# Second layer of a graph attention network on one core: tiles in ascending order of in-edges, a softmax in two halves for the largest three, and a later start of the next tile's softmax

## The chip, the cores and the metric

The kernel runs on one core of one Trainium2 chip, as one launch. The metric is the device time of that core in microseconds (us); less is better. The profile is of one execution, whose time is given beside the median.

## The reference, cut to what matters

A graph of 10000 nodes with 768 numbers each has 160000 edges, drawn at random in both directions, to which the kernel's input already adds one self loop for each node; the network adds another one. Two graph attention layers follow, with float32 throughout:

```python
def gat_conv(x, edge_index, W, a_src, a_dst, bias, heads, out_ch, concat):
    ei = _add_self_loops(edge_index, n)
    src, dst = (ei[0], ei[1])
    xl = (x @ W).reshape(n, heads, out_ch)
    e = leaky_relu(alpha_src[src] + alpha_dst[dst], 0.2)   # a dot of xl with a_src, a_dst
    m = jax.ops.segment_max(e, dst, num_segments=n)
    e = jnp.exp(e - m[dst])
    s = jax.ops.segment_sum(e, dst, num_segments=n)
    alpha = e / (s[dst] + 1e-16)
    msg = xl[src] * alpha[:, :, None]
    out = jax.ops.segment_sum(msg, dst, num_segments=n)
    return out + bias

h = layer_norm(gat_conv(x, ..., W1, HEADS=4, HID=256, concat), g1, be1)
h1 = relu(h) + (x @ Wr1 + br1)
h = layer_norm(gat_conv(h1, ..., W2, 1 head, OUT_DIM=768), g2, be2)
out = _layernorm(x + h + (h1 @ Wr2 + br2))
```

For each node, then, the rows of its in-neighbours are fetched, weighed by a softmax over their logits, and summed. In layer 2 such a row has 768 numbers, and two more for the logits.

## The kernel before

**Tiles and slots.** The kernel sorts the nodes by their number of in-edges and puts 128 of them, one on each partition, into each of 79 tiles (`NT`). A tile with at most n in-edges on a node has n slots, also called rows here: slot k of a tile holds the k-th in-neighbour of each of its 128 nodes, a transfer of 128 rows of 770 float32, 394 KB. The numbers of slots are fixed beforehand: 41, 27, 26, 25, 24 twice, 23 twice, 22 four times, 21 four times, 20 six times, 19 seven times, 18 seven times, 17 eight times, 16 seven times, 15 eight times, then fewer, down to 8; 1377 (`TOTAL`) in all. `SLOTS[t]` is the number of tile t, `FIRST[t]` its first slot.

**The order of the tiles.** Both layers go through the tiles in one order, every other size upwards and the remaining sizes downwards: 8, 10, 11 and so on up to 24, 26, 41, and then 27, 25, 24, 23 and so on down to 11, 11, 9. `TURNS[t]` is the place of tile t in the sorted list.

**Layer 2.** `ordered_layer2` keeps a ring of 41 slots (`RING2`) in SBUF. The instruction order of all engines is the program's own. `Ring.fetch` (L449) issues the transfer of a slot once the slot's former row has been used: slot 0 of a tile (the node's own row) by a plain DMA of SyncE (SP), every other by an indirect DMA of GpSimd (POOL), in `gather` (L424). 1298 gathers go through POOL's queue in this layer, and between them the 79 scatters of the results (L970). A gather whose slot is not yet free waits at the head of that queue.

For each tile of n rows, this is done:

- `weights_of` first makes the n logits and their exponentials (`logits`, L477 to L485; it needs all n rows in the ring), and at its second step the normalised weights (`normalised`, L496 to L499).
- Of each row, 512 columns are multiplied by the weight and summed on VectorE (DVE), one instruction a row (`weigh`, L519). The other 256 columns are summed in PSUM by TensorE (PE) with a diagonal matrix of the weights (L938); ScalarE (ACT) makes each diagonal from the identity (L937), in 5 buffers (`DIAGONALS`) of 4 diagonals each.
- `residual` (L949, L952) puts x and h1 @ Wr2 into other columns of the same PSUM tile; SP loads what it needs (L903, L904).
- `norms` makes the two layer norms: the deviation (`deviation`, L577 to L582, whose `sd` is made by ACT), then `scaled` (L591, L593) and the residual (L962), then the second deviation, the output (L968) and the scatter (L970). Its steps are issued in the next tile, ahead of row 0 and at rows 3, 6 and 9.

A row's ring slot is free when both the DVE's `weigh` and PE's diagonal matmul have read it.

**Where the next tile's softmax starts.** While tile t of n rows is weighed, the next tile's weights are made ahead. With `LEAD` = 3:

```python
if t + 1 < NT and SLOTS[t + 1] + LEAD <= ring.size:
    ahead = weights_of(t + 1)
    turn = min(max(n // 3, n + SLOTS[t + 1] + 2 * LEAD - ring.size), n - LEAD)
```

At row `turn` DVE's queue gets the next tile's logits, at row `turn` + 3 its normalised weights, and ACT and PE get its diagonals. A tile of 41 rows fills the whole ring, so its softmax is not made ahead: it comes after the last row of the tile before it.

Of the kernel before, what the change touches and what calls it, by code (L numbers as in the profile page):

```python
# [28 lines left out]
F32 = mybir.dt.float32  # L29
I32 = mybir.dt.int32  # L30
BF16 = mybir.dt.bfloat16
AF = mybir.ActivationFunctionType
# [13 lines left out]
G = 4  # L46
# [4 lines left out]
ON_PE2 = 512  # L51
SHARE = 4
ON_PE1 = 4


def chunk_counts(n_edges):
# [23 lines left out]
def gnn_kernel(ctx, tc, x, x_cols, src, dst, src_col, dst_col, W1, a_src1, a_dst1, b1, g1, be1, Wr1, br1,  # L80
# [342 lines left out]
    def gather(to, table, index, **more):  # L423
        nc.gpsimd.indirect_dma_start(out=to, out_offset=None, in_=table,  # L424
                                     in_offset=bass.IndirectOffsetOnAxis(ap=index, axis=0), **more)
# [14 lines left out]
    class Ring:  # L440
# [1 line left out]

        def __init__(self, pool, table, row, size, own):
            self.table, self.size, self.own, self.issued = table, size, own, 0
            self.rows = pool.tile([P, size, row], F32, name="ring")

        def fetch(self, upto):  # L449
            for q in range(self.issued, min(upto, TOTAL)):  # L450
                if q in self.own:
                    nc.sync.dma_start(self.slot(q), self.table[self.own[q] * P:(self.own[q] + 1) * P, :])
                elif q < self.size or self.own:
                    gather(self.slot(q), self.table[:, :], slots[:, q:q + 1])
                else:
                    gather(self.slot(q), self.table[:, :], slots[:, q:q + 1], bounds_check=NP - 1,
                           oob_is_err=False)
                self.issued = q + 1
# [12 lines left out]
    def logits(small, ring, lo, hi, ad, heads, c, top=None):  # L471


        n = hi - lo
        e = small.tile([P, ring.size, heads], F32, name="e")[:, :n]
        for a, b, rows in ring.parts(lo, hi):
            nc.vector.tensor_tensor(e[:, a - lo:b - lo], rows[:, :, c + heads:c + 2 * heads],  # L477
                                    ad[:, None, :].to_broadcast([P, b - a, heads]), op=OP.add)
        leaky(e, e)
        new = small.tile([P, heads], F32, name="new")  # L480
        nc.vector.reduce_max(new, e.rearrange("p k h -> p h k"), axis=AX.X)
        if top is not None:
            nc.vector.tensor_max(new, new, top)
        nc.vector.tensor_tensor(e, e, new[:, None, :].to_broadcast([P, n, heads]), op=OP.subtract)  # L484
        nc.scalar.activation(e, e, AF.Exp)  # L485
        for a, b, rows in ring.parts(lo, hi):
            if not ring.own:
                nc.vector.tensor_scalar(slots[:, a:b], rows[:, :, R1 - 1], -1.0, float(NP), op0=OP.mult, op1=OP.min)
                nc.vector.memset(rows[:, :, c + heads:], -BIG)
        return e, new  # L490

    def normalised(small, e, heads, t):

        doubled(e, t)
        total = small.tile([P, heads], F32, name="total")
        nc.vector.reduce_sum(total, e.rearrange("p k h -> p h k"), axis=AX.X)  # L496
        nc.vector.tensor_scalar(total, total, 1e-16, None, op0=OP.add)
        nc.vector.reciprocal(total, total)
        nc.vector.tensor_mul(e, e, total[:, None, :].to_broadcast([P, e.shape[1], heads]))  # L499
# [176 lines left out]


    SLOTS, FIRST = [SLOTS[t] for t in TURNS], [FIRST[t] for t in TURNS]

    def nodes(t):  # L680
        return order[:, TURNS[t]:TURNS[t] + 1]
# [195 lines left out]

    def ordered_layer2():
        nonlocal ps_big
        with tc.tile_pool(name="b2", bufs=1) as pool, tc.tile_pool(name="small2", bufs=2) as small, \  # L880
                tc.tile_pool(name="ps_acc2", bufs=2, space=PSUM) as ps_acc, \
                tc.tile_pool(name="ps_q2", bufs=3, space=PSUM) as ps_big, tc.manual_schedule():
# [1 line left out]
            wr2 = wr1.rearrange("p k n -> p (k n)")[:, :K1 * C2].rearrange("p (k n) -> p k n", n=C2)  # L884
            load(wr2, Wr2)
            parts = pieces(w2.rearrange("p k n -> p (k n)")[:, :6 * C1], C1)
            ring = Ring(pool, table2, R2, RING2, dict(zip(FIRST, TURNS)))

            rest, flat = RING2 * R2, ring.rows.rearrange("p k n -> p (k n)")

# [9 lines left out]
            def fetch_x(t):  # L900

                hT, xt = firsts[t] if t < 2 else (parts[t % 2], parts[2 + t % 2][:, :D0])
                nc.sync.dma_start(hT, h1_d[t])  # L903
                nc.sync.dma_start(xt, x_d[t])  # L904
                return hT.rearrange("p (k n) -> p k n", n=P), xt

            ins = {0: fetch_x(0)}
# [9 lines left out]
            ones = pool.tile([1, P], F32, name="ones")  # L917
            nc.vector.memset(ones, 1.0)

            def whole(t):  # L920
                return SLOTS[t] <= ring.size

            def weights_of(t):


                n = SLOTS[t]
                ad = small.tile([P, H2], F32, name="ad")
                nc.vector.tensor_add(ad, ring.slot(FIRST[t])[:, C2:C2 + H2], lift)
                e, _ = logits(small, ring, FIRST[t], FIRST[t] + n, ad, H2, C2)
                yield e  # L930
                normalised(small, e, H2, t)
                to = rs[t][:, C2:2 * C2 - ON_PE2]
                nc.tensor.matmul(to, ones, b2_b[0:1, ON_PE2:], start=False, stop=False, skip_group_check=True)
                for k in range(n):
                    if k % G == 0:
                        diagonals = pool.tile([P, G, P], F32, name="diagonals", bufs=DIAGONALS)
                    nc.scalar.activation(diagonals[:, k % G, :], ident, AF.Copy, scale=e[:, k, :])  # L937
                    nc.tensor.matmul(to, diagonals[:, k % G, :], ring.slot(FIRST[t] + k)[:, ON_PE2:C2],  # L938
                                     start=False, stop=(k == n - 1), skip_group_check=True)
                yield  # L940

            def residual(t):

# [13 lines left out]
            def norms(t, h, r, means):  # L957

                stats = deviation(small, [a for m in means for a in pieces(m, C2 - ON_PE2)])
                yield  # L960
                scaled(h, means, stats, g2_b, be2_b)
                nc.vector.tensor_add(h, h, r[:, :C2])  # L962
                mean, inv = deviation(small, pieces(h, C2 // 2))
                yield
                less = small.tile([P, 1], F32, name="less")
                nc.vector.scalar_tensor_tensor(less, mean, -1.0, inv, op0=OP.mult, op1=OP.mult)
                o = pool.tile([P, C2], F32, name="out")
                nc.scalar.activation(o, h, AF.Identity, bias=less, scale=inv)  # L968
                yield
                nc.gpsimd.indirect_dma_start(  # L970
                    out=out, out_offset=bass.IndirectOffsetOnAxis(ap=nodes(t), axis=0),
                    in_=o, in_offset=None, bounds_check=N - 1, oob_is_err=False)

            assert C2 % BANK and C2 % BANK + C2 - ON_PE2 <= BANK
            q = product(brT, wr2, C2)
            rs = {0: residual(0)}
            last = iter(())
            ready = []
            assert all(whole(t) for t in range(NT))
            for t in range(NT):  # L980
                n = SLOTS[t]
                if 0 < t < NT - 1:
                    rs[t + 1] = residual(t + 1)
                h = parts[4 + t % 2][:, :C2]
                e = (ready or list(weights_of(t)))[0]
                acc = ps_acc.tile([P, BANK], F32, name="acc")
                if not t:
                    rs[1] = residual(1)
                    ring.fetch(RING2)
                next(last, None)  # L990
                ready, ahead, turn = [], iter(()), n
                if t + 1 < NT and SLOTS[t + 1] + LEAD <= ring.size:

                    ahead = weights_of(t + 1)
                    turn = min(max(n // 3, n + SLOTS[t + 1] + 2 * LEAD - ring.size), n - LEAD)
                for k in range(n):
                    if k in (turn, turn + LEAD):
                        ready += itertools.islice(ahead, 1)
                    if k in (LEAD, 2 * LEAD, 3 * LEAD):
                        next(last, None)  # L1000
                    weigh(acc, ring.slot(FIRST[t] + k), e[:, k], ON_PE2, None if k else b2_b)
                    ring.fetch(FIRST[t] + k + 1 + ring.size)
                    if t + 2 < NT and k == n // 2:
                        ins[t + 2] = fetch_x(t + 2)
                ready += ahead
                for _ in last:
                    pass
                if not t:
                    nc.vector.tensor_add(be2_b, be2_b, adds[1])
                    nc.vector.tensor_add(be2_b, be2_b, q[:, :C2])  # L1010
                last = norms(t, h, rs[t], [acc, rs[t][:, C2:2 * C2 - ON_PE2]])
                if t + 2 < NT and t + 2 not in ins:
                    ins[t + 2] = fetch_x(t + 2)
# [272 lines left out]
```

## Time and profile before

| | |
|---|---|
| times of three runs | 5635.85, 5646.04 and 5645.9 us, median 5645.9 |
| the profiled execution's own time | 5629.25 us |
| its span in the profile | 5627.4 us, granted TensorE clock 0.927 |
| busy over the span | PE 87%, DVE 76%, POOL 58%, ACT 50% |
| layer 2 | from about 3437 us to the end, 2190 us |
| the group of 26, 41 and 27 rows | 4461.3 to 4631.4 us, 170.1 us |
| the five tiles ahead of it | 4283.8 to 4461.3 us, 177.5 us |

All windows below are counted from the start of the span. The profiled execution is 16.7 us below the median. PE's large share of busy time comes from layer 1 and its products more than from layer 2, so shares over the whole span don't tell what bounds layer 2.

### The profile page before, as it was taken

The numbers are of one execution on the slowest core, as the hardware profiler recorded it, in microseconds if no ns is written. First come the engines' busy times: TensorE is split into PE (matmuls) and PEld (weight loads), VectorE is DVE, ScalarE is ACT, GpSimd is POOL, SyncE is SP. The second block draws the span as 40 slices with busy tenths as digits, with TensorE's granted clock in tenths as the row PEclk, the third lists the DMA queues.
The fourth block names the chain that finished last, engine by engine and source line by source line (L and its number), as shares of the span: only waits on it lengthen the run. The fifth ranks groups of instructions, "written<-read, shape, count | busy, mean of one in ns | idle before, by whom it ended". The sixth has DMA issues, their size and how long they took to land. (4 is left out here: it accounts for less than half of the span.)

```text
span 5627.4 us, 59568 instructions
## 1 busy us (share of the span) xinstructions
PE 4889.5 (87%) x15191; PEld 2895.8 (51%) x15191; DVE 4288.7 (76%) x7729; ACT 2810.9 (50%) x8184; POOL 3236.3 (58%) x3159
## 2 busy tenths in 40 slices
PE   8999996999999875789999999998887747788898
PEld 3444443555555543455555555565555534555565
DVE  5783344999998887888999995887676656767787
ACT  3443343777788776778877763332222222222232
POOL 2447364556666555566665543666565656666663
PEclk9999998999999987899999999998888878889999
DMA  4333626999999987899999986998888878888885
GB/s 155 122 99 87 92 89 243 327 338 350 361 363 364 347 318 263 317 346 357 366 356 354 337 292 246 330 337 313 294 301 286 282 242 291 307 300 305 304 328 201
DMA packets 474306, 1591.37 MB, mean 283 GB/s; under 512 B 118327, under 2 KB 122487, under 8 KB 473958
## 3 DMA queue, kind: packets, MB, share of 16 engines
q0 software_dynamic: 322384, 1286.62, 64.5%
q1 hardware_dynamic: 149520, 297.43, 15.7%
q10 hardware_dynamic: 2054, 3.42, 0.2%
q8 instruction: 128, 2.10, 0.1%
q14 instruction: 220, 1.80, 0.1%
HBM read 1431.80 MB, written 177.29 MB: 286 GB/s over the span
## 5 line engine op out<-in xcount | busy, mean ns | idle before, releaser
L424 POOL DMA_INDIRECT ring<-table,slots x2675 | 2655.8, 993 | 1791.0 <-issue 518.8
L519 DVE SCALAR_TENSOR_TENSOR acc<-ring,e,acc 128x512 f32<-128x512 f32 (+1 forms) x2530 | 1578.4, 624 | 148.0 <-PE acc L733 48.6
L508 ACT ACTIVATE ring<-ring,e 128x256 f32<-128x256 f32 x3284 | 1338.6, 508 | 1.4 <-issue 1.4
L515 DVE TENSOR_TENSOR acc<-acc,ring 128x1024 f32<-128x1024 f32 x801 | 985.6, 1230 | 71.4 <-DVE acc L519 1.4
L952 PE MATMUL big<-wr,w 128*128 128x512 f32 (+1 forms) x2464 | 878.9, 502 | 139.8 <-issue 137.9
L938 PE MATMUL big<-ring,diagonals 128*128 128x256 f32 x2754 | 742.1, 428 | 206.0 <-issue 159.2
L171 PE MATMUL big<-w,xT 128*128 128x512 f32 x1896 | 825.9, 597 | 27.0 <-DMA w<-in_W_dram 10.4
L171 PE MATMUL big<-wr,xT 128*128 128x512 f32 x1896 | 833.5, 596 | 0.2 <-issue 0.2
L826 PE MATMUL half<-w,hT 128*128 128x512 f32 (+1 forms) x2528 | 830.4, 486 | 0.0
L938 PEld LDWEIGHTS big<-ring,diagonals 128*128 128x128 f32 x2754 | 586.4, 216 | 364.9 <-issue 232.7
L952 PEld LDWEIGHTS big<-wr,w 128*128 128x128 f32 x2464 | 482.3, 197 | 499.9 <-issue 468.9
L937 ACT ACTIVATE diagonals<-ident,e 128x128 f32<-128x128 f32 x1377 | 424.3, 388 | 617.2 <-remote 227.0
L826 PEld LDWEIGHTS half<-w,hT 128*128 128x128 f32 x2528 | 477.8, 189 | 372.3 <-issue 333.2
L733 PE MATMUL acc<-ring,diagonals 128*128 128x256 f32 x1912 | 481.8, 410 | 209.4 <-ACT diagonals L727 203.8
L171 PEld LDWEIGHTS big<-w,xT 128*128 128x128 f32 x1896 | 362.0, 192 | 486.6 <-issue 466.3
L171 PEld LDWEIGHTS big<-wr,xT 128*128 128x128 f32 x1896 | 356.7, 192 | 420.6 <-issue 420.5
L733 PEld LDWEIGHTS acc<-ring,diagonals 128*128 128x128 f32 x1912 | 388.8, 206 | 295.4 <-ACT diagonals L727 225.0
L581 ACT ACTIVATE sd<-mv,eps 128x1 f32<-128x1 f32 x237 | 69.4, 293 | 709.9 <-DVE mv L579 398.4
L727 ACT ACTIVATE diagonals<-ident,e 128x128 f32<-128x128 f32 x956 | 293.0, 387 | 204.2 <-DVE e L499 171.9
L665 DVE TENSOR_TENSOR scr<-big,ad_b 128x1024 f32<-128x1024 f32 x79 | 96.7, 1224 | 379.9 <-ACT row L662 348.1
L670 POOL TENSOR_TENSOR row<-row,none 128x1024 f32<-128x1024 f32 x79 | 187.1, 2368 | 266.6 <-ACT row L662 264.6
L485 ACT ACTIVATE e<-e 128x68 f32<-128x68 f32 (+29 forms) x160 | 38.2, 239 | 567.0 <-DVE e L484 302.0
(173 smaller groups left out, 3635.0 us busy)
## 6 DMA issues: line engine op xcount, KB each, us to landing
ring<-table,slots POOLq DMA_INDIRECT x2675
table<-row SPq DMA_DIRECT2D x79, 516.0 KB
h_d<-hT SPq DMA_DIRECT2D x79, 512.0 KB
w<-h_d SPq DMA_DIRECT2D x77, 512.0 KB
table<-row SPq DMA_DIRECT2D x79, 385.0 KB
ring<-table SPq DMA_DIRECT2D x79, 385.0 KB
xT<-in_x_cols_dram SPq DMA_DIRECT2D x79, 384.0 KB
x_d<-xt SPq DMA_DIRECT2D x79, 384.0 KB
```

The costliest lines, as they stand in the source:

```text
L171: nc.tensor.matmul(p[:, c:e], aT[:, j, :], w[:, j, c:e], start=(j == 0), stop=(j == k - 1))
L424: nc.gpsimd.indirect_dma_start(out=to, out_offset=None, in_=table, in_offset=bass.IndirectOffsetOnAxis(ap=index, axis=0), **more)
L508: nc.scalar.activation(row[:, s], row[:, s], AF.Copy, scale=e[:, h:h + 1])
L515: nc.vector.tensor_add(acc[:, :c], acc[:, :c], row[:, :c])
L519: nc.vector.scalar_tensor_tensor(acc[:, s], row[:, s], e[:, h:h + 1], (acc if first is None else first)[:, s], op0=OP.mult, op1=OP.add)
L670: nc.gpsimd.tensor_add(row[:, :C1], row[:, :C1], b1_b)
L727: nc.scalar.activation(diagonals[:, k * H1 + i, :], ident, AF.Copy, scale=e[:, k, i:i + 1])
L733: nc.tensor.matmul(acc[:, c:d], diagonals[:, k * H1 + i, :], ring.slot(q + k)[:, c:d], start=(k == 0 and c % BANK == 0), stop=(k == m - 1 ...
L826: nc.tensor.matmul(q, hT[:, j, :], w2[:, j, c:c + q.shape[1]], start=(j == 0), stop=(j == K1 - 1))
L937: nc.scalar.activation(diagonals[:, k % G, :], ident, AF.Copy, scale=e[:, k, :])
L938: nc.tensor.matmul(to, diagonals[:, k % G, :], ring.slot(FIRST[t] + k)[:, ON_PE2:C2], start=False, stop=(k == n - 1), skip_group_check=True)
L952: nc.tensor.matmul(r[:, c:d], hT[:, j, :], wr2[:, j, c:d], start=False, stop=(j == K1 - 1 and d < C2), skip_group_check=True)
```

## The change

Three things are changed, all in layer 2; layer 1 keeps its order and its code.

1. The tiles go from the fewest slots to the most: 8, 10, 11, 11, 9, 12 and so on up to 24, 24, and at the end 41, 25, 26, 27. (The two tiles that come last in layer 1 are sorted as if they had two slots more.) `Ring` gets a list `at` that maps the new order of slots to the columns of `slots`.
2. A tile of 26 or more rows (`PARTED2`) makes its softmax in two halves: 13 and 13, 20 and 21, 13 and 14 rows. After the first half the weights stay unnormalised; with the second half's maximum, `fade` rescales what both sums hold: ACT multiplies the 256 PSUM columns by it, and DVE the 512 columns of `acc` with one more instruction.
3. `turn` gets 4 * `LEAD` where it had 2 * `LEAD`, and counts the next tile's first half alone. For tiles of 18 rows it goes from row 6 to 7, of 19 from 6 to 9, of 20 from 6 to 11, of 21 from 7 to 13, of 22 from 9 to 15, of 23 from 11 or 12 to 17 and of 24 from 13 to 19. Up to 17 rows it stays where it was.

```diff
+PARTED2 = 26
...
-                    gather(self.slot(q), self.table[:, :], slots[:, q:q + 1])
+                    gather(self.slot(q), self.table[:, :], slots[:, self.at[q]:self.at[q] + 1])
...
     def ordered_layer2():
+        turns = sorted(range(NT), key=lambda t: SLOTS1[t] + 2 * (t >= NT - 2))
+        turns.insert(-3, turns.pop())
+        SLOTS = [SLOTS1[t] for t in turns]
+        FIRST = list(itertools.accumulate([0] + SLOTS[:-1]))
+        at = [FIRST1[t] + k for t in turns for k in range(SLOTS1[t])]
...
             def weights_of(t):
...
-                normalised(small, e, H2, t)
...
+                e, top = logits(small, ring, at, at + cuts[1], ad, H2, C2)
+                yield {0: (e, None)}
+                if len(cuts) == 2:
+                    normalised(small, e, H2, turns[t])
+                    add_b2()
+                else:
+                    doubled(e, turns[t])
+                    total = small.tile([P, H2], F32, name="total")
+                    nc.vector.reduce_sum(total, e.rearrange("p k h -> p h k"), axis=AX.X)
+                summed(e, 0, cuts[1])
                 yield
+                for lo, hi in zip(cuts[1:], cuts[2:]):
+                    e, new = logits(small, ring, at + lo, at + hi, ad, H2, C2, top)
+                    fade = small.tile([P, H2], F32, name="fade")
+                    nc.vector.tensor_sub(fade, top, new)
+                    nc.scalar.activation(fade, fade, AF.Exp)
+                    yield
...
+                    nc.vector.tensor_mul(e, e, total[:, None, :].to_broadcast([P, hi - lo, H2]))
+                    nc.scalar.activation(to, to, AF.Copy, scale=fade)
+                    add_b2()
+                    summed(e, lo, hi)
+                    yield lo, (e, fade)
...
-                    turn = min(max(n // 3, n + SLOTS[t + 1] + 2 * LEAD - ring.size), n - LEAD)
+                    turn = min(max(n // 3, cuts[-2] + 1, n + cuts_of(t + 1)[1] + 4 * LEAD - ring.size), n - LEAD)
                 for k in range(n):
+                    if k + LEAD in cuts[1:-1]:
+                        next(later)
+                    if k + 1 in cuts[1:-1]:
+                        lo, es_lo = next(later)
+                        es[lo] = es_lo
...
+                        if k == lo and fade is not None:
+                            nc.vector.scalar_tensor_tensor(acc[:, :ON_PE2], acc[:, :ON_PE2], fade, b2_b[:, :ON_PE2],
+                                                           op0=OP.mult, op1=OP.add)
```

More of the change, by code (lines that the diff above doesn't have):

```diff
@@ L440, in gnn_kernel, with __init__ @@
     class Ring:
-        def __init__(self, pool, table, row, size, own):
+        def __init__(self, pool, table, row, size, own, at=None):
             self.table, self.size, self.own, self.issued = table, size, own, 0
+            self.at = at or list(range(TOTAL))
             self.rows = pool.tile([P, size, row], F32, name="ring")
@@ L678, in gnn_kernel @@
     SLOTS, FIRST = [SLOTS[t] for t in TURNS], [FIRST[t] for t in TURNS]
+    SLOTS1, FIRST1 = SLOTS, FIRST
     def nodes(t):
@@ L886, in ordered_layer2 @@
             parts = pieces(w2.rearrange("p k n -> p (k n)")[:, :6 * C1], C1)
-            ring = Ring(pool, table2, R2, RING2, dict(zip(FIRST, TURNS)))
+            ring = Ring(pool, table2, R2, RING2, dict(zip(FIRST, (TURNS[t] for t in turns))), at)
             rest, flat = RING2 * R2, ring.rows.rearrange("p k n -> p (k n)")
@@ L902, in fetch_x @@
                 hT, xt = firsts[t] if t < 2 else (parts[t % 2], parts[2 + t % 2][:, :D0])
-                nc.sync.dma_start(hT, h1_d[t])
-                nc.sync.dma_start(xt, x_d[t])
+                nc.sync.dma_start(hT, h1_d[turns[t]])
+                nc.sync.dma_start(xt, x_d[turns[t]])
                 return hT.rearrange("p (k n) -> p k n", n=P), xt
@@ L918, in ordered_layer2, with cuts_of @@
             nc.vector.memset(ones, 1.0)
-            def whole(t):
-                return SLOTS[t] <= ring.size
+            def cuts_of(t):
+                n = SLOTS[t]
+                return [0, n // 2, n] if n >= PARTED2 else [0, n]
             def weights_of(t):
-                n = SLOTS[t]
+                n, at, cuts = SLOTS[t], FIRST[t], cuts_of(t)
                 ad = small.tile([P, H2], F32, name="ad")
-                nc.vector.tensor_add(ad, ring.slot(FIRST[t])[:, C2:C2 + H2], lift)
-                e, _ = logits(small, ring, FIRST[t], FIRST[t] + n, ad, H2, C2)
-                yield e
-                normalised(small, e, H2, t)
+                nc.vector.tensor_add(ad, ring.slot(at)[:, C2:C2 + H2], lift)
@@ L932, in weights_of @@
                 to = rs[t][:, C2:2 * C2 - ON_PE2]
[L933 to L939, printed above, removed]
@@ L940, in weights_of, with summed @@
-                yield
+                def summed(e, lo, hi):
+                    for k in range(lo, hi):
+                        if (k - lo) % G == 0:
+                            diagonals = pool.tile([P, G, P], F32, name="diagonals", bufs=DIAGONALS)
+                        nc.scalar.activation(diagonals[:, (k - lo) % G, :], ident, AF.Copy, scale=e[:, k - lo, :])
+                        nc.tensor.matmul(to, diagonals[:, (k - lo) % G, :], ring.slot(at + k)[:, ON_PE2:C2],
+                                         start=False, stop=(k == n - 1), skip_group_check=True)
@@ new lines, in add_b2 @@
+                def add_b2():
+                    nc.tensor.matmul(to, ones, b2_b[0:1, ON_PE2:], start=False, stop=False, skip_group_check=True)
+                e, top = logits(small, ring, at, at + cuts[1], ad, H2, C2)
[7 more added lines that the diff above has]
+                    nc.vector.reduce_sum(total, e.rearrange("p k h -> p h k"), axis=AX.X)
@@ new lines, in weights_of @@
+                summed(e, 0, cuts[1])
+                yield
+                for lo, hi in zip(cuts[1:], cuts[2:]):
[4 more added lines that the diff above has]
+                    yield
+                    part = small.tile([P, H2], F32, name="part")
+                    nc.vector.reduce_sum(part, e.rearrange("p k h -> p h k"), axis=AX.X)
+                    nc.vector.scalar_tensor_tensor(total, total, fade, part, op0=OP.mult, op1=OP.add)
+                    nc.vector.tensor_scalar(total, total, 1e-16, None, op0=OP.add)
+                    nc.vector.reciprocal(total, total)
+                    nc.vector.tensor_mul(fade, fade, total)
+                    nc.vector.tensor_mul(e, e, total[:, None, :].to_broadcast([P, hi - lo, H2]))
[3 more added lines that the diff above has]
+                    yield lo, (e, fade)
@@ L970, in norms @@
                 nc.gpsimd.indirect_dma_start(
-                    out=out, out_offset=bass.IndirectOffsetOnAxis(ap=nodes(t), axis=0),
+                    out=out, out_offset=bass.IndirectOffsetOnAxis(ap=nodes(turns[t]), axis=0),
                     in_=o, in_offset=None, bounds_check=N - 1, oob_is_err=False)
@@ L977, in ordered_layer2 @@
             last = iter(())
-            ready = []
-            assert all(whole(t) for t in range(NT))
+            ready, ahead = [], iter(())
+            assert max(SLOTS) <= ring.size
             for t in range(NT):
@@ L984, in ordered_layer2 @@
                 h = parts[4 + t % 2][:, :C2]
-                e = (ready or list(weights_of(t)))[0]
+                if not ready:
+                    ahead = weights_of(t)
+                    ready += itertools.islice(ahead, 2)
+                es, later, cuts = dict(ready[0]), ahead, cuts_of(t)
                 acc = ps_acc.tile([P, BANK], F32, name="acc")
@@ L991, in ordered_layer2 @@
                 ready, ahead, turn = [], iter(()), n
-                if t + 1 < NT and SLOTS[t + 1] + LEAD <= ring.size:
+                if t + 1 < NT:
                     ahead = weights_of(t + 1)
-                    turn = min(max(n // 3, n + SLOTS[t + 1] + 2 * LEAD - ring.size), n - LEAD)
+                    turn = min(max(n // 3, cuts[-2] + 1, n + cuts_of(t + 1)[1] + 4 * LEAD - ring.size), n - LEAD)
                 for k in range(n):
+                    if k + LEAD in cuts[1:-1]:
[3 more added lines that the diff above has]
+                        es[lo] = es_lo
                     if k in (turn, turn + LEAD):
@@ L1000, in ordered_layer2 @@
                         next(last, None)
-                    weigh(acc, ring.slot(FIRST[t] + k), e[:, k], ON_PE2, None if k else b2_b)
+                    lo = max(c for c in es if c <= k)
+                    weights, fade = es[lo]
+                    row = ring.slot(FIRST[t] + k)
+                    if k == 0 and len(cuts) > 2:
+                        nc.vector.tensor_scalar(acc[:, :ON_PE2], row[:, :ON_PE2], weights[:, 0], None, op0=OP.mult)
+                    else:
+                        if k == lo and fade is not None:
+                            nc.vector.scalar_tensor_tensor(acc[:, :ON_PE2], acc[:, :ON_PE2], fade, b2_b[:, :ON_PE2],
+                                                           op0=OP.mult, op1=OP.add)
+                        weigh(acc, row, weights[:, k - lo], ON_PE2, None if k else b2_b)
                     ring.fetch(FIRST[t] + k + 1 + ring.size)
@@ L1004, in ordered_layer2 @@
                         ins[t + 2] = fetch_x(t + 2)
-                ready += ahead
+                ready += itertools.islice(ahead, 2 - len(ready))
                 for _ in last:
```

## Prediction

> **What bounds the kernel now.** I read the page first, for the time and for the share of each engine, then the windows of layer 2, and within it the timelines and waits of POOL and DVE.
>
> ```profile
> span 5627.4 us, 59568 instructions
> PE 4889.5 (87%) x15191; PEld 2895.8 (51%) x15191; DVE 4288.7 (76%) x7729; ACT 2810.9 (50%) x8184; POOL 3236.3 (58%) x3159
> ...
> POOL 0%; issue 0%; POOLq 0%
> ```
>
> The chain of waits is almost empty: it only holds the last scatter. So it doesn't tell what bounds layer 2, and I work by stages. The windows give, after the time, the busy time and instructions of PE, PE's weight loads, DVE, ACT and POOL, then the granted clock, the DMA share and GB/s:
>
> ```profile
> 3437.00:5627.40 2190.40, 1791.84 (x5788) 1176.79 (x5788) 1586.36 (x3151) 594.89 (x1852) 1332.38 (x1377) 0.88 0.85 297
> 3530.60:3745.70 215.10, 201.08 (x703) 132.86 (x703) 189.46 (x398) 71.79 (x222) 145.18 (x148) 0.98 0.93 334
> 4283.80:4461.30 177.50, 127.74 (x399) 84.45 (x398) 118.88 (x226) 43.88 (x140) 114.20 (x119) 0.81 0.87 301
> 4461.30:4631.40 170.10, 100.33 (x326) 70.02 (x326) 91.99 (x164) 36.57 (x118) 86.94 (x92) 0.74 0.72 233
> 5558.20:5627.40 69.20, 49.64 (x174) 32.10 (x172) 47.22 (x96) 14.47 (x42) 4.80 (x5) 0.88 0.16 59
> ```
>
> The first line is the whole of layer 2, the second the small tiles of the rise, the third five tiles of 21 to 24 rows, the fourth the tiles of 26, 41 and 27 rows, the last the end after the last gather. With larger tiles, DVE's share falls from 0.88 to 0.67 and then 0.54, and the rate of transfers falls with it. POOL shows why:
>
> ```profile
> 4290.58 0.95 POOL L424 DMA_INDIRECT ring<-table,slots  x1 [0.30 <-issue]
> 4295.13 0.94 POOL L424 DMA_INDIRECT ring<-table,slots  x1 [3.60 <-PE big L938]
> ...
> 4300.54 0.95 POOL L424 DMA_INDIRECT ring<-table,slots  x1 [2.83 <-PE big L938]
> ...
> 4522.42 0.94 POOL L424 DMA_INDIRECT ring<-table,slots  x1 [14.91 <-DVE acc L519]
> ...
> 4538.27 0.94 POOL L424 DMA_INDIRECT ring<-table,slots  x1 [13.65 <-PE big L938]
> ```
>
> A gather that waits for nothing takes 0.95 us and a gap of 0.30. Over layer 2, 1332.4 us of POOL work and 1377 gaps of 0.30 (413) make 1745 of 2190 us; most of the rest is POOL waiting for a free slot, behind which every later gather queues. In an ordinary large tile these waits are of some 3 us; around the tile of 41, which needs the whole ring before its first row is weighed, two are of 14 to 15. DVE's waits in the same two windows are their shadow (us in total, times, longest):
>
> ```profile
> DVE w L593 <- ACT sd L582: 33.6, 4, 9.3
> POOL ring L424 <- PE big L938: 17.6, 9, 3.7
> DVE e L477 <- DMA ring<-table,slots: 15.5, 3, 7.6
> ```
>
> ```profile
> DVE e L477 <- DMA ring<-table,slots: 44.9, 4, 13.8
> POOL ring L424 <- DVE acc L519: 33.9, 15, 14.9
> POOL ring L424 <- PE big L938: 26.9, 6, 13.7
> ```
>
> The sum is made on the profiled execution (5629.25 us; the median is 16.7 above).
>
> **Step 1, the group of 26, 41 and 27.** POOL's work there is 86.94 + 92 × 0.30 = 114.5 us of 170.1, so it stands 55.6. The five ordinary tiles before it have 114.20 + 119 × 0.30 = 149.9 of 177.5: 27.6, or 5.5 a tile. Three tiles at 5.5 are 16.5, so the excess is 39.1 us. Halves remove its reason: 20 of 41 rows start the weighing, and freed slots refill while it goes on. The halves bring more breaks: I leave 41 rows one more pair of the waits above (3.60 + 2.83) and 26 one more 2.83, 9.3 in all. Gain 29.8. Bounds: 39.1, or 12 if two waits of 13.65 remain (39.1 − 27.3).
>
> **Step 2, the end.** The last gather ends at 5557.7 and the span 69.7 us later, for four tiles of 10, 11, 11 and 9 rows, each with its own norms. Afterwards the last gather goes into the slot that row 12 of the 26-row tile frees, so 14 rows of that tile and 27 rows remain. The gathers run behind the rows, so of those 14 rows (10.6 us) none or all may be left; I take half, 5.3. Then 1.2 for the gather, 27 × 0.756 = 20.4 for DVE's rows (L519 in the trace, with its gap), 6.2 for the 26-row tile's norms on DVE (its rows L577 to L966 at their mean durations), 2.9 for the second half's small operations, 3.6 for PE (DVE's wait for it ahead of the last deviation) and 19.5 from that deviation, at 5607.88, to the end: 59.1. Gain 10.6; the bounds are 15.9 (without the 5.3) and, if the whole 10.6, a second wait of 3.6 and one for `sd` of 8.4 remain, a loss of 6.7.
>
> **Step 3, added operations.** About ten small DVE operations (0.15 to 0.2 us each) and one of 128x512 (0.75) are 2.9 us for each halved tile; for the 27-row tile they stand in step 2. For the other two they lie beside POOL's pacing (DVE is busy 0.54 to 0.67 of the time there), so I cost them at 0; without that cover, 5.8. ACT gets nine more instructions, none over 0.5 us. The rescaling of PSUM waits for PE's first half, and behind it in ACT's queue stand the second half's diagonals and the next `sd`; rival B is this.
>
> **Step 4, the later softmax.** It moves logits, weights, diagonals and PE's 256-column matmuls of the next tile later in 32 tiles: by 1 row in seven tiles of 18, 3 in seven of 19, 5 in six of 20, 6 in four of 21 and four of 22, 5.5 in two of 23 and 6 in two of 24. That is 7 + 21 + 30 + 48 + 11 + 12 = 129 rows, at 0.756 us 97.5 us. No SP or POOL issue moves with it: `fetch` keeps its rows. For it: DVE's queue no longer stands at L477 before rows that have not landed (15.5 us in five tiles), behind which the current tile's `weigh` waits, and so POOL. Against it: a slot is free only when PE has read it too, and PE now begins the next tile two to five rows before DVE does. ACT makes 24 diagonals at 0.388 us (L937) in 9.3 us and PE multiplies them in 14.4 (L938 in that window: 65.0 us for 108 rows), against 18.1 for DVE's 24 rows, so PE keeps ahead once it has started. POOL is the pacer and 5.5 us a tile is all it waits today; so I take 0, as the two oppose each other. Bounds: a gain of 30 (those 15.5 us and as much again in the other large tiles), and a loss of 97.5.
>
> This window had a clock of 0.81, against 0.98 where PE is steadily fed. The Trainium skill ("TensorE: Matmul & The Clock Gate", Part 1) says that PE's clock halves after an idle window of about 3.4 us; that speaks against this edit, as PE would stand before the bundled diagonals and start them at half speed. By it each such burst would lose up to half of 3.4 us, an estimated 20 us over the twelve tiles of 21 to 24 rows, and the sum would be −20. The trace's clock agrees in direction; no row shows the gate itself.
>
> **Step 5, the order alone.** The same work in another order: where rise and fall have four tiles each of one size, they cost 87.9 and 84.5 us (15 rows) and 111.5 and 101.6 (17 rows). So 0, within 13 (3.4 + 9.9).
>
> Sum: −29.8 − 10.6 + 0 + 0 + 0 = −40: 5589 for the profiled execution, 5606 for the median.
>
> **The rivals.**
>
> A, slower: the late diagonals hold ACT. Before L593, DVE waits for ACT's `sd`, which stands behind the diagonals:
>
> ```profile
> 4473.04 1.02 DVE L593 SCALAR_TENSOR_TENSOR w<-w,sd,be 128x768 f32<-128x768 f32 x1 [8.38 <-ACT sd L582]
> ```
>
> If the diagonals take as long as now but start 129 rows later over the 32 tiles, all 97.5 us show in that wait: −40 + 97.5 = +57, 5703. It decides from 41% of that shift, 1.3 us a tile. For it: the wait is there today in four of five tiles. Against: in the tile's 18 us of rows there is time to catch up.
>
> B, the halves give back their gain: ACT's rescaling of PSUM and the second logits wait for the ring as the whole softmax did, so two waits of 13.65 remain (gain 12), and the end gains nothing and pays the 5.8 of step 3: −6, 5640. For it: `cuts` are fixed rows, and the 41 rows still exceed what the ring holds ahead. Against: the first half needs only 20 rows.
>
> C, a larger gain: the later softmax also takes away the 30 us of step 4, and step 1 its full 39.1, step 2 its full 15.9: −85, 5561. That "six rows later" is true only from 21 rows on speaks against more.
>
> **How the numbers follow.** Forecast 0.42, A 0.21, B 0.19, C 0.18. A change of 0.2%, 11.3 us, is about what a measurement can tell. Faster: 0.39 of the forecast, all of C and a third of B (0.06), 0.63. Same: the rest of the forecast's low gains and most of B, 0.15. Slower: A and a touch of B, 0.22. The range reaches from C (5561, with step 5's 13 below it 5548) to just short of A's full price, 5685, which leaves out the upper half of A and little of C.
>
> **What would show it.** Right: in layer 2 of the changed kernel no POOL wait of over 10 us; the end after the last gather is 50 to 63 us; ordinary large tiles keep 5.5 us of POOL waiting, within 1; L477's waits for gathers shrink in tiles of 21 to 24 rows. Wrong: L593's wait for `sd` grows beyond 10 us, or POOL's slot waits per large tile rise (A); waits of 13 us around the 41-row tile (B). A falling clock in the 21- to 24-row stretch would bear out the gate.

## The result, and the profile after

The changed kernel took 5603.28 us (median of four runs, 5597.98 to 5613.01), the kernel before beside it 5643.78: a ratio of 0.9936, 95% interval 0.9921 to 0.9952. The forecast was 5606, with a range of 5548 to 5685. The profiled execution took 5607.1 us with a span of 5605.3, against 5629.25 and 5627.4 before. Of these 22 us, 6.6 lie ahead of layer 2, in code that is the same in both (the first gather of layer 2 starts at 3434.7 instead of 3441.3), so the two traces show 15.5 us of layer 2 and the medians more. The prediction's sum was made on the profiled execution and gave 5589 for it; there the time is 18 us above it, while the medians agree.

The time of the kernel before differs between occasions, which must be known for what follows: it took 5644 and 5634 us on two of them and 5333, 5324 and 5323 us on three others. The experiments ran on four chips, each of them on one occasion, so I speak of slower and faster chips; that the chip itself makes the difference, and not something else of the occasion, is not shown. Each ratio below is to the kernel before on the same chip. The prediction was made and measured at the slower time.

The page, and windows of layer 2, of five ordinary tiles (one of 21 and four of 22 rows), of the tiles of 41, 25 and 26 rows, and of the end after the last gather (columns as before):

```profile
span 5605.3 us, 59627 instructions
PE 4888.6 (87%) x15188; PEld 2899.2 (52%) x15191; DVE 4294.8 (77%) x7761; ACT 2813.9 (50%) x8193; POOL 3242.1 (58%) x3159
```

Busy times are within 6.1 us of before on every engine; what changed is how long the engines stand.

```profile
3437.00:5605.30 2168.30, 1791.88 (x5786) 1180.99 (x5784) 1591.38 (x3182) 597.82 (x1860) 1330.74 (x1375) 0.89 0.86 299
...
5100.00:5267.70 167.70, 125.48 (x401) 84.29 (x401) 116.41 (x222) 41.97 (x135) 107.48 (x110) 0.84 0.85 295
5420.40:5557.00 136.60, 92.91 (x278) 60.72 (x277) 93.96 (x182) 33.87 (x109) 82.14 (x86) 0.78 0.81 278
5546.70:5605.30 58.60, 23.36 (x82) 18.37 (x82) 35.43 (x66) 11.86 (x36) 2.01 (x2) 0.67 0.08 31
```

The end after the last gather is 58.6 us instead of 69.7. Around the tiles of 41, 25 and 26 rows, the waits (us in total, times, longest) are now these, where L425 is the gather:

```profile
DVE e L479 <- DMA ring<-table,slots: 11.4, 1, 11.4
POOL ring L425 <- PE big L946: 8.1, 9, 4.1
POOL ring L425 <- remote: 7.0, 3, 4.1
POOL ring L425 <- DVE ad L938: 4.6, 1, 4.6
DVE w L595 <- ACT sd L584: 4.5, 1, 4.5
```

The two slot waits of 14.91 and 13.65 are gone; the longest of POOL in this window is 4.6. In the five ordinary tiles, however, one wait of DVE has taken the other's place:

```profile
DVE w L595 <- ACT sd L584: 45.6, 5, 9.4
POOL ring L425 <- issue: 23.8, 78, 0.3
POOL ring L425 <- remote: 14.7, 4, 3.8
POOL ring L425 <- PE big L946: 9.3, 5, 3.5
...
DVE e L479 <- issue: 0.4, 2, 0.2
```

The wait for gathers at the logits (L479; before, L477, 15.5 us in five tiles) has vanished, and the wait for `sd` (L595; before, L593) has grown from 33.6, in four of five tiles, to 45.6 in all five. In the tiles of 23 and 24 rows behind them it reaches more than the 10.1 us that it has at most in layer 2 of the kernel before:

```profile
5357.70 1.02 DVE L595 SCALAR_TENSOR_TENSOR w<-w,sd,be 128x768 f32<-128x768 f32 x1 [13.56 <-ACT sd L584]
...
5398.06 1.02 DVE L595 SCALAR_TENSOR_TENSOR w<-w,sd,be 128x768 f32<-128x768 f32 x1 [12.92 <-ACT sd L584]
```

### The profile page after: what moved, and what is told of

Same layout as the page of the kernel before. It is cut to its first block, busy times and chain, and to the rows that moved or that the text cites. A ratio compares the mean times of both kernels' runs of the same rounds, so it can differ in the third digit from the quotient of the medians.

```text
span 5605.3 us, 59627 instructions
## 1 busy us (share of the span) xinstructions
PE 4888.6 (87%) x15188; PEld 2899.2 (52%) x15191; DVE 4294.8 (77%) x7761; ACT 2813.9 (50%) x8193; POOL 3242.1 (58%) x3159
## 5 line engine op out<-in xcount | busy, mean ns | idle before, releaser
L425 POOL DMA_INDIRECT ring<-table,slots x2675 | 2660.2, 994 | 1774.4 <-issue 542.1
L172 PE MATMUL big<-w,xT 128*128 128x512 f32 x1896 | 823.8, 596 | 26.5 <-DMA w<-in_W_dram 10.3
L670 ACT ACTIVATE scr<-scr 128x256 f32<-128x256 f32 x632 | 253.6, 402 | 120.3 <-DVE scr L667 117.7
```

Of the source, the lines that this page charges most:

```text
L172: nc.tensor.matmul(p[:, c:e], aT[:, j, :], w[:, j, c:e], start=(j == 0), stop=(j == k - 1))
L670: nc.scalar.activation(m[:, s], m[:, s], AF.Copy, accum_out=row[:, C1 + i * H1 + h:C1 + i * H1 + h + 1])
```

## The experiments

My theory was that POOL's gathers pace layer 2, that halves and order are worth what the prediction said, and that the later softmax is neutral. The main rivals were that the order brings the gain, and that the later softmax costs or brings much. I took the three parts singly and in pairs. All edits are to the changed kernel; the first four experiments ran on a faster chip.

**Halves alone** (old order, old start of the softmax):

```diff
-        turns = sorted(range(NT), key=lambda t: SLOTS1[t] + 2 * (t >= NT - 2))
-        turns.insert(-3, turns.pop())
+        turns = list(range(NT))
...
-                    turn = min(max(n // 3, cuts[-2] + 1, n + cuts_of(t + 1)[1] + 4 * LEAD - ring.size), n - LEAD)
+                    turn = min(max(n // 3, cuts[-2] + 1, n + cuts_of(t + 1)[1] + 2 * LEAD - ring.size), n - LEAD)
```

> The old order and the old start of the next softmax, with the softmax of the tiles of 26, 41 and 27 rows in two halves. Theory (gathers pace layer 2 and the ring standing full around the 41-row tile is what the change removes): the two slot waits of 14 to 15 us around the 41-row tile go, 25 to 35 us faster than before, the end after the last gather stays at 70 us. Rival B (the halves give back what they gain): within 12 us of before. Rival C' (the later softmax or the order brings the gain): within 8 us of before.

5300.25 us against 5332.62, ratio 0.9940 (0.9926 to 0.9953), 32 us faster. As the theory had it.

**Order alone** (`PARTED2 = 99`; a tile of 41 rows is then not made ahead, as before; old start):

```diff
-PARTED2 = 26
+PARTED2 = 99
...
-                if t + 1 < NT:
+                if t + 1 < NT and cuts_of(t + 1)[1] + LEAD <= ring.size:
...
-                    turn = min(max(n // 3, cuts[-2] + 1, n + cuts_of(t + 1)[1] + 4 * LEAD - ring.size), n - LEAD)
+                    turn = min(max(n // 3, cuts[-2] + 1, n + cuts_of(t + 1)[1] + 2 * LEAD - ring.size), n - LEAD)
```

> The new order alone: ascending, 41, 25, 26, 27 at the end, each with a whole softmax, the next softmax where it was. Theory: only the end gets shorter, from 70 to about 58 us, and the waits of 14 to 15 us around the 41-row tile stay: 5 to 15 us faster than before. Rival (the order is what brings the gain, by a steadier ring): 30 to 45 us faster. Rival (the end is made longer by one large tile): slower by 5 to 15.

Same chip: 5340.23 us, ratio 1.0016 (1.0007 to 1.0025): 8 us slower, against my 5 to 15 faster. The end after the last gather is 59.0 us (66.7 with halves in the old order), as expected; ahead of it some 16 us are lost (8 + 7.7). POOL's timeline of this kernel still has the two waits around the 41-row tile:

```profile
5161.28 0.95 POOL L425 DMA_INDIRECT ring<-table,slots  x1 [15.15 <-DVE acc L521]
...
5177.37 0.95 POOL L425 DMA_INDIRECT ring<-table,slots  x1 [13.88 <-PE big L946]
```

With halves alone, the waits of POOL in the window of 24, 26, 41 and 27 rows stay far below them:

```profile
POOL ring L425 <- DVE acc L521: 8.8, 20, 1.1
POOL ring L425 <- PE big L945: 7.7, 24, 0.7
```

**Later softmax alone** (old order, whole softmaxes):

```diff
-PARTED2 = 26
+PARTED2 = 99
...
-        turns = sorted(range(NT), key=lambda t: SLOTS1[t] + 2 * (t >= NT - 2))
-        turns.insert(-3, turns.pop())
+        turns = list(range(NT))
...
-                if t + 1 < NT:
+                if t + 1 < NT and cuts_of(t + 1)[1] + LEAD <= ring.size:
```

> The old order and whole softmaxes, the next tile's softmax later by up to six rows in tiles of 18 and more rows. Theory (it is neutral, as POOL paces the tiles): within 10 us of before. Rival A (the diagonals hold ACT's sd): 20 to 97 us slower, with longer waits of L595 for sd. Rival C (it takes away waits for landed rows): 15 to 30 us faster.

Same chip: 5290.10 us, ratio 0.9925 (0.9911 to 0.9938): 42 us faster. The theory said neutral; it is rival C's gain, on this chip, and larger. The last experiments show its mechanism.

**Order and halves, without the later softmax:**

```diff
-                    turn = min(max(n // 3, cuts[-2] + 1, n + cuts_of(t + 1)[1] + 4 * LEAD - ring.size), n - LEAD)
+                    turn = min(max(n // 3, cuts[-2] + 1, n + cuts_of(t + 1)[1] + 2 * LEAD - ring.size), n - LEAD)
```

> The changed kernel with the next softmax back where it was (two LEADs instead of four); new order and halves stay. Theory: within 10 us of the changed kernel, so 30 to 50 us faster than before. Rival A: the later softmax cost something, and this is 10 to 30 us faster than the changed kernel, 50 to 70 faster than before. Rival C: it brought something, and this is 10 to 30 us slower than the changed kernel, 10 to 30 faster than before.

Same chip: 5303.77 us, ratio 0.9948 (0.9935 to 0.9962), 28 us faster, below the theory's 30 to 50 and within rival C's 10 to 30. It is 4 us short of halves alone, which the two intervals do not tell apart.

The next four ran on a slower chip. There the times of the kernel before spread from 5624 to 5658 us, and the ratios lie up to 0.001 below the quotients of the medians.

**The changed kernel again:** no edit.

> The changed kernel as it is, beside the runs before it. Theory now (the later softmax brings some 40 us here and the halves some 30, and they add up, less the 8 that the order costs): 55 to 65 us faster than the kernel before. Rival (both take away the same slot waits): 35 to 45 us faster.

5610.12 us against 5634.0, ratio 0.9950 (0.9931 to 0.9970): 28 us faster (17 to 39 by the interval), far from the 55 to 65 of added parts; the rival's 35 to 45 is only touched.

**Order and later softmax, whole softmaxes:**

```diff
-PARTED2 = 26
+PARTED2 = 99
...
-                if t + 1 < NT:
+                if t + 1 < NT and cuts_of(t + 1)[1] + LEAD <= ring.size:
```

> The changed kernel with whole softmaxes: new order, later start. Theory (the parts add up): 25 to 35 us faster than before. Rival (both take away the same waits): 35 to 45 us faster, as the changed kernel.

5640.53 us, ratio 1.0004 (0.9991 to 1.0016): no change, where both expectations had 25 to 45 us. So without the halves nothing of the gain is left: on this chip they are worth (1.0004 − 0.9950) × 5634 = 30 us, the difference of two ratios that are each known to 7 to 11 us. POOL again has the two waits (14.2 us for DVE and 13.1 for PE).

**Halves and later softmax, old order:**

```diff
-        turns = sorted(range(NT), key=lambda t: SLOTS1[t] + 2 * (t >= NT - 2))
-        turns.insert(-3, turns.pop())
+        turns = list(range(NT))
```

> The changed kernel in the old order of tiles: halves and the later start. Theory (the parts add up, and the order costs some 8): 65 to 75 us faster than before, so faster than the changed kernel. Rival (the order is needed for the halves to bring anything, as the end is shorter): slower than the changed kernel by 5 to 15.

5623.08 us, ratio 0.9971 (0.9958 to 0.9984): by this 16 us faster than before, where the theory had 65 to 75, and slower than the changed kernel, as the rival said. By this the order is worth (0.9971 − 0.9950) × 5634 = 12 us here. The two intervals overlap; the end after the last gather, 69.5 us against 59.7 in the traces, speaks for it. The group of 26, 41 and 27 rows, in the old order as before, now takes 140.0 us where it took 170.1:

```profile
4460.20:4600.20 140.00, 95.81 (x287) 61.82 (x287) 97.72 (x198) 35.45 (x115) 90.65 (x96) 0.78 0.88 303
```

**The kernel before, traced again:** no edit.

> The kernel before as it is, for its trace beside the others: slot waits of some 2 us in an ordinary tile of 20 to 24 rows and two of 13 to 15 around the 41-row tile, the end after the last gather 66 to 70 us. If instead the ordinary tiles wait 5 us each, the lower time of the last runs has come from their own change and not from the chip.

5629.72 us, and in ordinary tiles of 21 and 22 rows POOL waits 6.9 and 5.4 us each (the sum of what its gaps exceed 0.30); the end is 70.1 us. I had expected some 2 us in an ordinary tile. This chip is another than that of the first four experiments, and the kernel before took 5634 us on it, so their low times came from their chip or occasion and not from their edits.

The next three ran on another faster chip.

**The changed kernel a third time:** no edit.

> The changed kernel as it is, so that the next two stand beside it on one chip. Theory: where the kernel before takes some 5640 us, 25 to 40 us faster than it, as twice before; where it takes some 5330 us, 55 to 70 us faster, as halves and later softmax each brought 30 to 40 there.

5256.43 us against 5324.22, ratio 0.9870 (0.9855 to 0.9885): 68 us faster. Halves (−32), later softmax (−42) and order (+8), measured on the first of the faster chips, add up to −66.

**Without the later softmax, again:** the edit of the fourth experiment.

> The changed kernel with the next softmax where it was. Theory (the later softmax pays only where POOL is otherwise unhindered): where the kernel before takes some 5640 us, within 10 us of the changed kernel; where it takes some 5330 us, 25 to 40 us slower than the changed kernel. Rival A: faster than the changed kernel by 10 to 30 us where before takes 5640. Rival C: slower than it by 15 to 30 us on either.

5296.63 us, ratio 0.9948 (0.9935 to 0.9962): 40 us slower than the changed kernel. The same 16 tiles of 20 to 23 rows, first without the later softmax, then with it; first the windows, then the waits:

```profile
4608.10:5074.50 466.40, 379.13 (x1280) 264.05 (x1279) 364.78 (x701) 136.84 (x438) 324.69 (x341) 0.89 0.93 333
```

```profile
4602.70:5034.60 431.90, 371.40 (x1280) 258.92 (x1279) 364.76 (x701) 132.11 (x425) 327.76 (x340) 0.92 0.97 359
```

```profile
DVE e L479 <- DMA ring<-table,slots: 83.5, 16, 6.6
POOL ring L425 <- DVE acc L521: 53.5, 69, 4.2
```

```profile
DVE e L479 <- DMA ring<-table,slots: 46.9, 15, 5.9
...
POOL ring L425 <- DVE acc L521: 16.0, 52, 0.5
```

Work is the same (DVE 364.8 us in both), the stretch 34.5 us shorter. Without the later start, the logits stand 5 us a tile at the head of DVE's queue until the next tile's last row lands; meanwhile no `weigh` frees a slot, and POOL comes to stand for it (53.5 us, up to 4.2 at a time). With it, the logits still stand 3 us a tile, but POOL's longest such wait is 0.5. Counted as in step 1, POOL stands 466.4 − 324.69 − 341 × 0.30 = 39.4 us without the later start and 2.1 with it. These 37 us are about what the stretch is shorter: gathers follow each other almost without a break.

**Seven buffers of diagonals:**

```diff
-DIAGONALS = 5
+DIAGONALS = 7
```

> The changed kernel with 7 buffers of diagonals instead of 5, so that ACT can make the 21 to 24 diagonals of a tile without waiting for PE to give one back, and the sd behind them comes sooner. Theory (the slots' release by PE sets the pace, and DVE's wait for sd is its shadow): within 8 us of the changed kernel, with DVE's wait for sd in tiles of 21 to 24 rows smaller by half. Rival A (diagonals that hold ACT are a cost): 15 to 50 us faster than the changed kernel where it has waits of 9 us for sd in these tiles.

5258.94 us, ratio 0.9873 (0.9858 to 0.9888): as the changed kernel on the same chip. There, the wait for `sd` is at most 2.7 us with five buffers already, so this says nothing on the waits of 9 us of the slower chips; whether more buffers help there was not tried.

**The first 40 tiles interleaved**, on a third of the faster chips:

```diff
         turns.insert(-3, turns.pop())
+        turns[:40] = [turns[i + j] for i in range(20) for j in (0, 20)]
```

> The changed kernel with the first 40 tiles (8 to 17 rows) interleaved, a small one after a larger one: 8, 15, 10, 15, 11, 15 and so on. Theory (where POOL is unhindered, tiles of up to 14 rows in a row are DVE's and larger ones POOL's, and the ring of 41 slots can even out two neighbours): where the kernel before takes some 5330 us, POOL's slot waits in the tiles of 9 to 14 rows (some 20 us in the changed kernel) go and it is 76 to 86 us faster than before, 8 to 18 faster than the changed kernel. Where before takes some 5640 us: within 10 us of the changed kernel, so 20 to 45 us faster than before. Rival (the waits in small tiles come from the start of the ring or from the loads of SP and not from DVE): within 5 us of the changed kernel on either.

5254.86 us against 5322.91, ratio 0.9869 (0.9852 to 0.9885): no better than the changed kernel's 0.9870, where I had expected 8 to 18 us. POOL's waits in the tiles of 9 to 14 rows fell from 18 to 6 us, but those in the tiles of 15 to 17 rows, now between them, rose from 5 to 10. The window of these tiles shows why nothing follows:

```profile
3483.00:4046.00 563.00, 563.00 (x2007) 374.67 (x2006) 534.60 (x1123) 196.57 (x615) 418.18 (x433) 1.00 0.99 374
```

DVE is busy 0.95 of the time and PE 1.00: small tiles are not short of gathers in this order, nor in the changed kernel's (0.94 and 0.99 from 3472.5 to 4018 us). What the order costs ahead of the end on the faster chips is spread over many tiles and stays open.

## Why the prediction was right, and where it was lucky

**Step 1, the group of large tiles: right.** Predicted 29.8 us; the halves are worth 30 on a slower and 32 on a faster chip, each the difference of kernels that have and lack them. In the old order the trace of the seventh experiment has the group itself shorter by 30.1 us (170.1 to 140.0), though the 25-row tile behind it takes 6.6 us more. In the trace of the changed kernel POOL waits 11.6, 3.2 and 3.8 us in the tiles of 41, 25 and 26 rows, an excess of only 2.1 over 3 × 5.5, where I had left 9.3. Rival B's two waits of 13.65 are gone, and with them Rival B.

**Step 2, the end: right in sum, by two misses that cancel.** Predicted 59.1, measured 58.6 and 59.7; the order as a whole is worth 12 us on the slower chip (step 2 said 10.6). By its terms, DVE after the last gather:

```profile
5548.29 0.76 DVE L579 BATCH_NORM_STATS2 st<-acc 128x6 f32<-128x256 f32 x2
5556.35 0.43 DVE L579 BATCH_NORM_STATS2 st<-big 128x6 f32<-128x256 f32 x1 [7.30 <-PE big L946]
...
5585.79 0.42 DVE L579 BATCH_NORM_STATS2 st<-big 128x6 f32<-128x256 f32 x1
```

The rest of the 26-row tile was only two rows, 1.5 us where I had 5.3, but PE came 7.30 us late where I had 3.6: from the last gather's end at 5546.7 to the last tile's first row at 5557.0 it is 10.3 us, against 5.3 + 1.2 + 3.6. That the two misses cancel is luck. I had put the wait for PE ahead of the last deviation, at the very end; it came ahead of the 26-row tile's, and the last tile has none. From 5585.79 to the end it is 19.5, as the old end had it.

**Step 3, the added operations: right where the trace shows them.** In the second half of the 27-row tile the small operations and the rescaling take DVE 2.7 us (from 5569.05 to 5574.03, less three rows), where I had 2.9. That they cost nothing in the other two tiles was not tried by itself.

**Step 4, the later softmax: no change to be seen on the slower chip, by another balance than the step gave.** The 32 tiles of 18 to 24 rows take 1009 us before (993 in its second trace), 1005 after (1004 in its second), and 998 in the seventh experiment, which has the old order: no difference beyond that of the two traces of before. The step set the logits' waits against a late start of PE. What came instead is rival A's wait. In these 32 tiles, DVE stands 39.9 and 37.8 us ahead of the logits in the two traces of before and 4.8 and 6.2 in the two of after; ahead of L593 (now L595) it stands 91.7 and 79.1 us before and 119.5 and 120.0 after. So the wait for `sd` did grow, by 28 to 41 us of rival A's 97.5, about as much as the logits' waits shrank. Two marks set for A came true: waits for `sd` of over 10 us, three of them up to 13.6 (and one ahead of L595 that the profile puts down to nothing), where before had one of 10.1; and POOL's waits in the tiles of 24 rows, 4.8 and 5.3 us a tile in the two traces of before and 7.8 to 10.1 in the four on slower chips with the later start.

The changed kernel without the later start was not run on a slower chip. If the three parts add up, its ratios there give the later start as a loss of (1.0004 + 0.9971 − 1 − 0.9950) × 5634 = 14 us (19 by the medians), known to some 15. So the 0 of this step is neither shown nor refuted there to better than that.

On the faster chips the same edit is worth 40 and 42 us, beyond the 30 that I gave as the most it could bring. The logits' waits are larger there: 119.5 us in the 32 tiles without the later start and 77.8 with it, while the waits for `sd` only go from 3.3 to 7.0 and the tiles' time falls by 39.3. The bound was read in a trace that held a third of these waits. The whole gain of 68 us comes near rival C's 85 by another sum: 32 + 42 − 8 for its 39.1 + 30 + 15.9.

**Step 5, the order alone: at the edge of its 13.** On the slower chip the order's 12 us are the end's 10 and little else. On a faster chip the gathers from first to last take 1803.6 us with halves alone and 1816.8 with the order added, a loss of 13 ahead of the end; without the halves it is some 16.

**The sum.** −40 was forecast. The medians differ by 40 us on the first occasion and 24 on the second; the ratios give 36 (27 to 45 by the interval) and 28 (17 to 39). That the first medians meet the forecast within 1 us is luck in part.

**The clock.** The granted clock of the ordinary large tiles did not fall: 0.84 after against 0.81 before, and on a faster chip 0.92 with the later softmax against 0.89 without. The rule of the Trainium skill ("TensorE: Matmul & The Clock Gate", Part 1) that idle windows halve the clock is not tested by these averages; the 20 us estimated from it did not show.

Of the marks set for the forecast, no POOL wait for a slot above 10 us (the longest is 8.8), the end of 50 to 63 us and the shrunken waits of L479 came true. The 5.5 us of POOL's waiting stayed in tiles of 21 and 22 rows (5.8 and 5.4), but not in those of 23 and 24 rows, with 7.6 (8.3 before) and 10.1.

## What to carry to other kernels

Where one queue paces a stage, count its work, then price each edit by the queue's own waits in the stretch that the edit touches; a wait of another engine is worth only what the queue gets of it. An instruction that waits for data should be queued as late as its consumer allows, since everything behind it on its engine, and every buffer that these would free, waits with it. And a bound read in a trace with a second limiter in it holds for that limiter only: the same edit brought nothing that could be seen on one chip and 40 us on another.

## What the runs showed of the hardware that I had not expected

The time of this kernel differs by some 5.5% between chips (as far as chip and occasion can be told apart), nearly all of it in layer 2: from the first `weigh` to the end the kernel before takes 2168.9 us on a slower chip, while the first gather starts at 3435.1 there and at 3431.3 with the order-only kernel on a faster one, where the layer takes 1879.9. On the slower chips PE's releases come late. In the trace of before, PE's matmuls run until 4286, then hardly at all until 4294.66:

```profile
4284.21 1.24 PE L938 MATMUL big<-ring,diagonals 128*128 128x256 f32 x5
4286.24 0.38 PE L938 MATMUL big<-ring,diagonals 128*128 128x256 f32 x1 [0.80 <-issue]
4289.06 0.51 PE L938 MATMUL big<-ring,diagonals 128*128 128x256 f32 x1 [2.44 <-issue]
...
4294.66 2.06 PE L938 MATMUL big<-ring,diagonals 128*128 128x256 f32 x4 [0.82 <-issue]
```

By the trace's record of semaphores (the counters by which engines tell each other that a step is done), no increment by PE arrives in that time, and then eleven in 0.45 us, from 4294.68 on, just as the gathers' queue runs dry (it moved 314 KB in the last microsecond but one before, 129 KB in the last, and nothing in the three after). POOL's gather at 4295.13 was waiting for them, and ACT's longest wait for PE (L937) in these five tiles is 15.1 us. Such bunches of four and more increments within 0.1 us of each other occur 71 to 85 times in layer 2 in each of the six traces on slower chips, and not once in the eight on faster ones, where an increment follows the start of its row's second matmul by 0.18 us (median; in the trace of before by 0.61, and by 10 or more in one of twenty). That the held increments make these chips slower fits this; what holds them, no run here shows.

On a faster chip the transfers reach 374 GB/s over the 563 us shown above. The Trainium skill ("DMA: Bandwidth & Descriptors", its opening table) gives some 358 GB/s as HBM's limit for a core, half of what two cores share; this stretch, with the gathers reading HBM and one core at work, lies above it.
